# A sparse two-layer graph attention kernel: one transposition or one projection per step, with the copies a step later, and two runs of chunks as one access

## The chip, the cores and the metric

The kernel runs on 1 core of one Trainium2 chip. The core has a matrix engine (TensorE, PE in the profile; its weight loads are PEld), a vector engine (VectorE, DVE), an activation engine (ScalarE, ACT), a general engine (GpSimd, POOL) and a queue for plain transfers (SyncE, SP). Each works through its own instructions in the order in which the program issues them, and waits for others by semaphores. The metric is device time in microseconds (us) for the whole program.

## The reference

4096 nodes with 512 features; a random adjacency whose rows thin out from node 0 on. Twice: graph attention, a residual and a layernorm.

```
def attention(x, W, a):            # 8 heads of 64, or one of 512
    h = x @ W                      # per head
    e = leaky_relu(f_dst[:, None] + f_src[None, :], 0.2)
    e = where(adj > 0, e, -inf)
    return softmax(e) @ h

x = layernorm(x + attention_8(x, W0, a0))
h = elu(attention_8(x, W1, a1))              # 8 heads, concatenated
h = elu(attention_1(h, Wo, ao))              # one head of 512
x = layernorm(x + relu(h @ lin1_w + lin1_b) @ lin2_w + lin2_b)
```

Below, layer 1 and layer 2 are the two attentions of 8 heads, layer 3 is the attention of one head with the two dense products behind it. Everything is computed in fp32.

## The kernel before, in words

The nodes are cut into 32 tiles of 128. A first phase (to about 312 us of the span) turns the adjacency into lists: for each tile but the first, its edges are sorted into chunks of 128 (one edge per partition), with a source row to gather and a target node in the tile. It also projects the input for layer 1. A dense version of the program stands by for graphs that do not fit the lists; it does not run here.

Each attention reads a table in DRAM: one row per node, with its projected features and its scores. `heads_layer` (L1679) runs layers 1 and 2. Its loop (L1767) goes over *units* of up to 6 chunks; one pass is a *step*. A tile has one to five units; light tiles (17 to 31) and heavy ones (1 to 16) alternate. For a unit:

- `gather` (L1340): GpSimd issues one indirect DMA per chunk, five units ahead.
- `weights` (L1429): VectorE adds the target's and the source's scores into `z` and takes the leaky relu (L1442 to L1445), ScalarE writes two exponentials, `g` and `wp` (L1447, L1456). A unit has one or two runs of neighbouring chunks, and each run had its own instruction (`pick`, L1298). `wp` has one PSUM buffer, so that its exponential waits until the scaling of the unit before has read it.
- `scale` (L1487): VectorE builds the masks `sm` of edges against nodes (L1507 in layers 1 and 2, one instruction for each half of the tile) and multiplies the gathered rows by `wp` (L1526).
- `sum` (L1528): TensorE adds the unit's rows into the tile's accumulator (L1548).

Tile 0 is nearly full and is done densely: `First.make` (L1596) prepares one block of 128 source nodes on ScalarE (2 + 8 + 8 activations, L1607 to L1612), `sort_out` masks it on VectorE (L1620), `add` sums two blocks on TensorE (L1634) at the first step of every second tile (`taken`, L1776). These sums are called F here, and the time from one F to the next a *cycle*: 14 of them in a layer, most with one light and one heavy tile. A block's rows are loaded on the SP queue (L1592).

When a tile's units are summed, it goes through a chain of its own, kept in the list `ways`: `divide` (VectorE: reciprocal, product, and the residual with the layernorm's statistics in layer 1; ScalarE: two small activations of the layernorm, or in layer 2 two exponentials of elu, L1656 and L1657), `norm` (VectorE finishes; TensorE transposes the tile, 4 matmuls, L714; ScalarE copies the transposed tile to `xt`, 4 activations with their accumulators, L717), `project` (TensorE, L726: two halves into two PSUM tiles `ph`), `rows` (ScalarE copies the halves to `hrow`, L753, and the scores, L760; a store to the next table on the SP queue, L754). `row_of_s` (L778) spreads the scores of tile 0 over all partitions for the next layer; its `make` needs them. `split` prepares scores for the next layer. The transposed tile `pt` and the two halves `ph` share one tag with two PSUM buffers, so a transposition needs a buffer that `rows` has read out, and a projection one that the copies of `xt` have read out.

Short names for these pieces, used from here on: T (transposition), X (copies to `xt`), P (projection), H (the copies of `rows`), S (the sums of a unit), M (a `make`), N (the layernorm's two small activations).

In the loop before, a step runs `spread` and `fetch` (first step of a tile), then P, `weights` of the next unit, M, `scale`, F and `divide` (if taken), S, `gather`, H, `sort_out`, T with X, `divide`. After the loop one tile is left; `mean_of_all_but` (L798) and `finish_mean` (L818) write the mean row of the next table, then the next layer's gathers can start.

Of the kernel before, what the change touches and what calls it, by code (L numbers as in the profile page):

```python
# [11 lines left out]
F32 = mybir.dt.float32  # L12
# [4 lines left out]
AF = mybir.ActivationFunctionType  # L17
OP = mybir.AluOpType
# [4 lines left out]
P = 128  # L23
# [6 lines left out]
FC = F // P  # L30
# [10 lines left out]
HN = P // 2  # L41
# [519 lines left out]
def sparse_path(  # L561
# [24 lines left out]
    nc = tc.nc  # L586
# [16 lines left out]
    ident = const.tile([P, P], F32, name="s_ident")  # L603
# [12 lines left out]
    iota_n = const.tile([P, P], F32, name="iota_n")  # L616
# [8 lines left out]
    nl = const.tile([P, total], F32, name="nl")  # L625
# [84 lines left out]
    def turn_in(sb, ps, st, src, t):  # L710

        pt = ps.tile([P, FC, P], F32, name="pt", tag="ph")
        for c in range(FC):
            nc.tensor.transpose(pt[:, c, :], src[:, ts(c, P)], ident)  # L714
        xt = sb.tile([P, FC, P], F32, name="xt")
        for c in range(FC):
            nc.scalar.activation(  # L717
                xt[:, c, :], pt[:, c, :], AF.Copy, accum_out=st.xparts[:, c, t : t + 1]
            )
        return xt  # L720
# [559 lines left out]
    class Unit:  # L1280
# [17 lines left out]
        def pick(self, a, base=0):  # L1298

            at = 0  # L1300
            for first, n in self.runs:
                yield slice(at, at + n), a[:, first - base : first - base + n]
                at += n

    class Whole:


# [25 lines left out]
    class Attention:  # L1333
# [99 lines left out]
        def scores(self, u):  # L1433

            hs = self.st.heads
            if u.t == 0:
                return self.weights_of_first(u)
            base = parts_of(u.t)[0].first
            z = self.wk.tile([P, GC, hs], F32, name="z")[:, : u.n]
            d = by_head(u.g[:, : u.n])[:, :, :, DM] if hs > 1 else u.g[:, : u.n, F + 1 : self.st.row]  # L1440
            for at, s in u.pick(self.s[u.t], base):
                nc.vector.tensor_add(z[:, at], s, d[:, at])  # L1442
            nc.vector.scalar_tensor_tensor(z, z, ALPHA, z, op0=OP.mult, op1=OP.max)
            for at, ls in u.pick(self.ls[u.t], base):
                nc.vector.tensor_sub(z[:, at], z[:, at], ls)  # L1445
            if hs > 1:
                nc.scalar.activation(d, z, AF.Exp)  # L1447
            u.z = z
# [38 lines left out]
        def scale(self, u):  # L1487

            if u.t == 0:
                return  # L1490
            hs, n = self.st.heads, u.n
            if u.first:
                left = [sum(p.chunks[h] for p in pts if p.t == u.t) for h in range(2)]
                self.seen[u.t] = [0, 0], left

            sm = self.wk.tile([P, most_slots, HN], F32, name="sm")
            node = {k: nl[:, c : c + 1] for k, c in enumerate(u.chunks)}
            seen, left = self.seen[u.t]
            todo, at = [], 0
            for g, slots in enumerate(u.slots):  # L1500
                of_g = iota_n[:, g * HN : (g + 1) * HN]
                if hs > 1 and slots:
                    k, n_ = slots[0], len(slots)
                    c = u.chunks[k]
                    assert u.chunks[k : k + n_] == list(range(c, c + n_))
                    shape = [P, n_, HN]
                    nc.vector.tensor_tensor(  # L1507
                        sm[:, at : at + n_],
                        of_g[:, None, :].to_broadcast(shape),
                        nl[:, c : c + n_, None].to_broadcast(shape),  # L1510
                        op=OP.is_equal,
                    )
                for i, k in enumerate(slots):
                    if hs == 1:
                        nc.vector.tensor_scalar(  # L1515
                            sm[:, at + i], of_g, node[k], u.w[:, k], op0=OP.is_equal, op1=OP.mult
                        )
                    seen[g] += 1
                    todo.append((i, g, k, at + i, seen[g] == 1, seen[g] == left[g]))
                at += len(slots)  # L1520
            todo.sort(key=lambda x: x[:2])
            u.todo, u.sm = todo, sm
            if hs > 1:
                body = u.g[:, :n].rearrange("p n (h w) -> p (n h) w", w=HD)[:, :, :DM]
                wp = u.wp[:, :n].rearrange("p n h -> p (n h)")
                nc.vector.tensor_mul(body, body, wp[:, :, None].to_broadcast(body.shape))  # L1526
# [152 lines left out]
    def heads_layer(gp, wk, sb, pp, st, nxt, fetch, finish, clear):  # L1679
# [5 lines left out]
        order = [t for pair in zip(range(NT - 1, NT // 2, -1), many) for t in pair] + [1]  # L1685
# [5 lines left out]
        with tc.tile_pool(name=f"ha_{st.name}", bufs=2, space=PSUM, reuse_waits="tile") as pacc, \  # L1691
# [3 lines left out]
            at = Attention(st, gp, wk, pacc, one, whole)  # L1695
            extra = {}
            if clear:
                for i in range(GB):
                    g = gp().rearrange("p k f -> p (k f)")
# [21 lines left out]
            def divide_first():  # L1721
                at.inverse(sb, 0)
                o = at.normal(sb, 0, spare())
                finish(o, 0, extra.pop(0))()
                return norm, 0, o, lambda: None
# [4 lines left out]
            def divide(t):  # L1730
                at.inverse(sb, t)
                o = at.normal(sb, t)
                return norm, t, o, finish(o, t, extra.pop(t))

            def norm(t, o, rest):
                rest()
                xt = turn_in(pp, ps, nxt, o, t)
                return project, t, xt

            def project(t, xt):  # L1740
# [13 lines left out]
            def split(lo, n):  # L1754
                split_s(pp, nxt, lo, n)

            def run(of):

                mine = [way for way in ways if way[0] is of]
                for way in ([w for w in mine if w[1] != 0] or mine)[:1]:  # L1760
                    ways.remove(way)
                    nxt_ = of(*way[1:])
                    if nxt_:
                        ways.append(nxt_)

            ways, out_, resting = [], set(), None
            for i, u in enumerate(units):  # L1767
                pos = order.index(u.t)
                spread = None
                if u.first and pos + 2 < NT - 1:  # L1770
                    spread = at.spread(order[pos + 2])
                    extra[order[pos + 2]] = fetch(order[pos + 2])
                run(project)
                if i + 1 < len(units):
                    at.weights(units[i + 1])
                taken = u.first and first.sorted - first.summed >= min(DB, NT - first.summed) > 0  # L1776
                if i > 0:
                    first.make(i)
                held = None
                at.scale(u)  # L1780
                first.take()
                if taken:
                    first.add(DB)
                    held = divide(order[pos - 1]) if pos > 0 else None
                    if first.summed == NT:
                        extra[0] = fetch(0, spare())
                        resting = i + 2
                at.sum(u)
                if i + GB < len(units):
                    at.gather(units[i + GB])  # L1790
                late_split = [way for way in ways if way[0] is split]
                run(rows)
                run(row)
                if first.sorted < first.made - 1 or first.made == NT:
                    first.sort_out()
                run(norm)
                if held:
                    ways.append(held)
                elif u.first and pos > 0:
                    ways.append((divide, order[pos - 1]))  # L1800
                    run(divide)
                if i == resting:
                    ways.append(divide_first())
                if spread:
                    spread()
                if late_split:
                    run(split)
            assert resting and resting < len(units) - 4
            assert all(way[0] is split for way in ways)
            ways.append((divide, order[-1]))  # L1810
            run(divide)
            mrow = mean_of_all_but(pp, ps, nxt, order[-1])
            while ways:
                for of in (project, rows, row, split, norm, divide):
                    run(of)
                    if of is rows and len(out_) == NT:
                        finish_mean(ps, nxt, mrow)

# [3 lines left out]
    with ExitStack() as pools:  # L1822
        big = pools.enter_context(tc.tile_pool(name="eb", bufs=1))
        sb = pools.enter_context(tc.tile_pool(name="es", bufs=2))
        ps = pools.enter_context(tc.tile_pool(name="ep", bufs=1, space=PSUM))
        pp = pools.enter_context(tc.tile_pool(name="eq", bufs=2, space=PSUM))
# [85 lines left out]
    pp = layers.enter_context(tc.tile_pool(name="lp", bufs=2, side="right", reuse_waits="tile"))  # L1912
# [30 lines left out]
    with tc.tile_pool(name="ta", bufs=2, space=PSUM, reuse_waits="tile") as pacc, \  # L1943
# [9 lines left out]
        order = [t for block in blocks for t in block]  # L1953
        units = units_of(order)
        units[:1] = units[0].cut(2)
        at = Attention(st2, lambda: keep.tile([P, GC, F + HS], F32, name="g"), wk, pacc, ps)
# [379 lines left out]
```

## Time and profile before

| | us |
|---|---|
| median of 9 runs (lowest to highest) | 1931.04 (1928.01 to 1933.0) |
| the profiled execution | 1925.58 |
| its span, first to last instruction | 1923.8 |

| engine | busy us | share of the span |
|---|---|---|
| TensorE, matmuls | 1627.5 | 85% |
| VectorE | 1354.1 | 70% |
| GpSimd | 999.1 | 52% |
| ScalarE | 909.1 | 47% |

The span falls into the lists (0 to about 312 us), layer 1 (to 778), layer 2 (to 1208) and layer 3. In layer 1 TensorE is busy 384.5 of 466 us and VectorE 394.4; in layer 2 TensorE 366.0 of 430 us and VectorE 315.6. The mean clock granted to TensorE is 0.935 of full speed over the span.

In groups of instructions, "x1536 | 393.2, 410" means 1536 records, 393.2 us in all, 410 ns each; one matmul of the program shows as several records. In a timeline a line gives the start in us, the time from the first start to the last end of a merged run, the engine, the line of the program, and in brackets how long the engine stood idle before and who released it. Ends of matmuls are modelled, and runs of them overlap a little.

### The profile page before, as it was taken

How to read it: one execution, taken by the hardware profiler on the slowest of the kernel's cores; microseconds unless marked ns; L12 is line 12 of the kernel's file. 1: busy time of each engine (PE TensorE's matmuls, PEld its weight loads, DVE VectorE, ACT ScalarE, POOL GpSimd, SP SyncE). 2: the span in 40 equal slices, each digit the busy share in tenths (PEclk: the TensorE clock that was granted, in tenths of full speed). 3: DMA queues.
4: the chain of work that ended last, by engine and by line, in shares of the span. 5: the costliest groups of instructions: out<-in, count | busy, mean ns of one | idle time of the engine just before them, and what ended most of it. 6: DMA issues, size and time to landing. Idle time of an engine off the chain costs nothing.

```text
span 1923.8 us, 31095 instructions
## 1 busy us (share of the span) xinstructions
PE 1627.5 (85%) x9797; PEld 1205.9 (63%) x9797; DVE 1354.1 (70%) x3537; ACT 909.1 (47%) x3294; POOL 999.1 (52%) x1336
## 2 busy tenths in 40 slices
PE   4998877788988887688898988589899998899987
PEld 1675555566666665356666665366678666667776
DVE  6787666889898888388887776245665766656665
ACT  5986877555455645276666653112223131222311
POOL 5556565766665563477776563644405454535100
PEclk8999988789998998789999999789899999999999
DMA  9798873767776665467776663744545544435111
GB/s 327 282 333 312 290 269 118 224 201 214 213 230 196 203 192 175 132 179 198 196 200 185 181 164 110 240 112 116 145 142 158 131 121 140 109 119 154 56 45 35
DMA packets 140084, 343.69 MB, mean 179 GB/s; under 512 B 39525, under 2 KB 44653, under 8 KB 132230
## 3 DMA queue, kind: packets, MB, share of 16 engines
q0 software_dynamic: 64064, 180.85, 34.4%
q1 hardware_dynamic: 74246, 156.57, 23.5%
q10 hardware_dynamic: 1600, 4.19, 0.6%
q8 instruction: 80, 1.31, 0.3%
q14 instruction: 94, 0.77, 0.1%
HBM read 332.19 MB, written 42.24 MB: 195 GB/s over the span
## 4 chain that ended last, share of the span: by engine, by line
PE 40%; DVE 15%; issue 12%; POOL 10%; ACT 8%; DMA 6%; POOLq 0%; DVEq 0%; ACTq 0%; SPq 0%
PE ph L726 10%; PE acc L1548 10%; POOL g L1350 9%; DMA g<-table_t,idx 6%; DVE g L1526 3%; PE acc L1634 3%; PE px L2063 3%; PE px L2071 2%; PE py L2063 2%; ACT w L1610 2%; PE pz L2063 2%; ACT rows L1612 1%; PE py L2071 1%; PE acc L1478 1%; PE pz L2071 1%
## 5 line engine op out<-in xcount | busy, mean ns | idle before, releaser
L1350 POOL DMA_INDIRECT g<-table_t,idx x774 | 815.5, 1054 | 620.2 <-PE acc L1548 271.5
L1548 PE MATMUL acc<-g,sm 128*64 128x260 f32 (+2 forms) x3408 | 466.0, 406 | 106.9 <-DVE sm L1515 55.2
L1548 PEld LDWEIGHTS acc<-g,sm 128*64 128x64 f32 x3408 | 266.2, 144 | 269.7 <-DVE sm L1515 75.6
L726 PE MATMUL ph<-sw_t,xt 128*128 128x264 f32 (+1 forms) x1536 | 393.2, 410 | 35.5 <-ACT xt L717 28.7
L726 PEld LDWEIGHTS ph<-sw_t,xt 128*128 128x128 f32 x1536 | 303.2, 202 | 105.7 <-ACT xt L717 40.5
L1526 DVE TENSOR_TENSOR g<-g,wp 128x2048 f32<-128x2048 f32 (+5 forms) x114 | 291.8, 2560 | 1.9 <-ACT wp L1456 1.9
L717 ACT ACTIVATE xt<-pt 128x128 f32<-128x128 f32 x256 | 67.0, 276 | 197.2 <-PE pt L714 197.2
L1610 ACT ACTIVATE w<-s_row,d 128x128 f32<-128x128 f32 x512 | 155.8, 387 | 0.0
L1634 PE MATMUL acc<-rows,w 128*128 128x65 f32 x1024 | 125.3, 283 | 12.3 <-ACT rows L1612 12.3
L1634 PEld LDWEIGHTS acc<-rows,w 128*128 128x128 f32 x1024 | 125.2, 201 | 15.0 <-ACT rows L1612 12.8
L1158 DVE MAX8 cand<-key 128x8 f32<-128x85 f32 (+51 forms) x395 | 99.8, 317 | 44.2 <-PE key L992 44.1
L1612 ACT ACTIVATE rows<-rows 128x64 f32<-128x64 f32 x512 | 128.6, 334 | 0.0
L977 ACT ACTIVATE sg<-raw,value 128x2048 bf16<-128x2048 int32 x60 | 120.1, 2008 | 4.3 <-DMA raw<-in_adj_dram 3.9
L2077 ACT ACTIVATE shid<-shid,sl1b 128x256 f32<-128x256 f32 x112 | 50.6, 500 | 118.3 <-DVE shid L2015 118.3
L1667 ACT ACTIVATE rstd<-mv,s_eps 128x1 f32<-128x1 f32 x64 | 18.9, 295 | 143.8 <-DVE mv L1664 143.8
L714 PE MATMUL pt<-s_ident,o 128*128 128x128 f32 x248 | 42.7, 297 | 48.2 <-ACT ss_t L760 48.2
L1620 DVE SCALAR_TENSOR_TENSOR w<-w,mask 128x1024 f32<-128x1024 f32 x64 | 77.6, 1214 | 7.6 <-ACT w L1610 7.6
L1658 DVE SCALAR_TENSOR_TENSOR o<-ex,o 128x512 f32<-128x512 f32 x63 | 43.4, 689 | 52.5 <-ACT ex L1657 52.5
L1656 ACT ACTIVATE ex<-o 128x512 f32<-128x512 f32 x63 | 39.6, 629 | 76.1 <-DVE o L1574 67.4
L714 PEld LDWEIGHTS pt<-s_ident,o 128*128 128x128 f32 x248 | 27.3, 146 | 74.6 <-ACT ss_t L760 58.4
L1515 DVE TENSOR_SCALAR sm<-iota_n,nl,w 128x64 f32<-128x64 f32 x284 | 68.7, 318 | 0.0
L1459 ACT ACTIVATE w<-z 128x4 f32<-128x4 f32 (+4 forms) x56 | 11.6, 206 | 115.1 <-DVE z L1445 108.6
(284 smaller groups left out, 2824.7 us busy)
## 6 DMA issues: line engine op xcount, KB each, us to landing
raw<-in_adj_dram SPq DMA_DIRECT2D x60, 1024.0 KB, 7.9
table_t<-hrow SPq DMA_DIRECT2D x64, 260.0 KB, 4.0
rows<-table_t SPq DMA_DIRECT2D x64, 260.0 KB, 4.1
xr<-in_x_dram SPq DMA_DIRECT2D x63, 256.0 KB, 4.9
g<-table_t,idx POOLq DMA_INDIRECT x774, 3.8
table_t<-hrow SPq DMA_DIRECT2D x32, 257.0 KB, 4.6
xr<-sx_d SPq DMA_DIRECT2D x32, 256.0 KB, 3.1
out_dram<-xr SPq DMA_DIRECT2D x32, 256.0 KB, 2.8
```

Source lines behind the costliest of these rows:

```text
L726: nc.tensor.matmul(ph[:n], columns(c), st.w[:, c, j], start=(c == 0), stop=(c == FC - 1))
L977: nc.scalar.activation(sg[:, ts(i, w)], raw[:, ts(i, w)], AF.Sign, bias=values["half"])
L1158: nc.vector.max(out=cand[:, at : at + 8], in_=key[:, j - w0_ : j - w0_ + n_])
L1350: nc.gpsimd.indirect_dma_start(out=u.g[:, k, : self.st.row], out_offset=None, in_=self.st.table[:, :], in_offset=bass.IndirectOffsetOnAxis ...
L1526: nc.vector.tensor_mul(body, body, wp[:, :, None].to_broadcast(body.shape))
L1548: nc.tensor.matmul(out_[g * HN : (g + 1) * HN], sm[:, slot], rows(k), start=start, stop=stop)
L1610: nc.scalar.activation(w[:, h], self.st.s_row[:, h], AF.Exp, scale=0.8, bias=d8[:, h : h + 1])
L1612: nc.scalar.activation(rows[:, h, :DM], rows[:, h, :DM], AF.Copy, scale=rows[:, h, DM : DM + 1])
L1620: nc.vector.scalar_tensor_tensor(w, w, 1.0, mask0[:, self.turns[b], None, :].to_broadcast([P, HS, P]), op0=OP.max, op1=OP.mult)
L1634: nc.tensor.matmul(acc[:, j, k * HD : (k + 1) * HD], w[:, h], rows[:, h * HD : (h + 1) * HD], start=(b == lo and k == 0), stop=(b == hi - ...
L2063: nc.tensor.matmul(out_[:, m], a[:, c, ts(k, P)], b[:, c], start=m == 0 and c == 0, stop=k == ks[-1] and c == 1,)
L2071: nc.tensor.matmul(out_[:, :HF], a[:, k, ts(r, P)], b[:, k], start=k == 0, stop=k == 3)
```

## The change

Three things change; line numbers in the diff are those of the old and new file.

1. The chain of a tile in `heads_layer`. `norm` only transposes; the copies to `xt` are a stage of their own, `turned`. In a step, `turned`, `rows` and `row` come after the next unit's weights and the make, ahead of `scale`. Behind the step's sums comes either one projection or, if none is ready, one transposition. `make_room` keeps at most one tile waiting for its transposition: when a tile is about to be divided and another still waits, it runs the outstanding `rows` and `turned` and transposes, in the same step. In steps that take two blocks of tile 0 it is called between F and S. After the loop, what is left is drained.
2. The input rows for the residual (`fetch`) are asked for at the end of a tile's first step, behind the spread, and not at its start.
3. Where a unit has two runs of chunks, the additions and subtractions on `z` (all three layers) and the masks `sm` (layers 1 and 2, where each half of the tile has its own run) are one instruction with one more dimension (`both_runs`).

```diff
+    def both_runs(a, u, base=0):
+        (one, n), (two, m) = u.runs
+        assert n == m and two > one
+        v = a[:, one - base : one - base + n]
+        step, lanes, *rest = [list(x) for x in v.ap][1], v.ap[0], *[list(x) for x in v.ap][2:]
+        return bass.AP(v.tensor, v.offset, [list(lanes), [step[0] * (two - one), 2], step, *rest])
...
+            if len(u.runs) == 2:
+                z_, d_ = (a.rearrange("p (r k) h -> p r k h", r=2) for a in (z, d))
+                nc.vector.tensor_add(z_, both_runs(self.s[u.t], u, base), d_)
+            else:
+                for at, s in u.pick(self.s[u.t], base):
+                    nc.vector.tensor_add(z[:, at], s, d[:, at])
...
+            whole_ = hs > 1 and len(u.runs) == 2
+            if whole_:
+                k = n // 2
+                shape = [P, 2, k, HN]
+                nc.vector.tensor_tensor(
+                    sm[:, :n].rearrange("p (g k) w -> p g k w", g=2),
+                    iota_n.rearrange("p (g w) -> p g w", g=2)[:, :, None, :].to_broadcast(shape),
+                    both_runs(nl, u)[:, :, :, None].to_broadcast(shape),
+                    op=OP.is_equal,
+                )
...
             def norm(t, o, rest):
                 rest()
-                xt = turn_in(pp, ps, nxt, o, t)
+                pt = ps.tile([P, FC, P], F32, name="pt", tag="ph")
+                for c in range(FC):
+                    nc.tensor.transpose(pt[:, c, :], o[:, ts(c, P)], ident)
+                return turned, t, pt
+
+            def turned(t, pt):
+                xt = pp.tile([P, FC, P], F32, name="xt")
+                for c in range(FC):
+                    nc.scalar.activation(
+                        xt[:, c, :], pt[:, c, :], AF.Copy, accum_out=nxt.xparts[:, c, t : t + 1]
+                    )
                 return project, t, xt
...
+            def make_room():
+                made = False
+                while sum(way[0] is norm for way in ways) > 1:
+                    while run(rows):
+                        pass
+                    while run(turned):
+                        pass
+                    run(norm)
+                    made = True
+                return made
...
                     spread = at.spread(order[pos + 2])
-                    extra[order[pos + 2]] = fetch(order[pos + 2])
-                run(project)
                 if i + 1 < len(units):
                     at.weights(units[i + 1])
...
                     first.make(i)
-                held = None
+                late_split = [way for way in ways if way[0] is split]
+                run(turned)
+                run(rows)
+                run(row)
+                held, made_room = None, False
                 at.scale(u)
                 first.take()
                 if taken:
                     first.add(DB)
+                    made_room = make_room()
                     held = divide(order[pos - 1]) if pos > 0 else None
...
                 at.sum(u)
                 if i + GB < len(units):
                     at.gather(units[i + GB])
-                late_split = [way for way in ways if way[0] is split]
-                run(rows)
-                run(row)
                 if first.sorted < first.made - 1 or first.made == NT:
                     first.sort_out()
-                run(norm)
+                if not made_room and not run(project):
+                    run(norm)
                 if held:
                     ways.append(held)
                 elif u.first and pos > 0:
+                    make_room()
                     ways.append((divide, order[pos - 1]))
                     run(divide)
                 if i == resting:
+                    make_room()
                     ways.append(divide_first())
                 if spread:
                     spread()
+                    extra[order[pos + 2]] = fetch(order[pos + 2])
...
-            assert all(way[0] is split for way in ways)
+            make_room()
             ways.append((divide, order[-1]))
             run(divide)
+            while any(way[1] != order[-1] for way in ways if way[0] in (norm, turned)):
+                for of in (project, rows, row, split, norm, turned):
+                    while run(of, False) and of in (rows, turned):
+                        pass
             mrow = mean_of_all_but(pp, ps, nxt, order[-1])
             while ways:
-                for of in (project, rows, row, split, norm, divide):
-                    run(of)
+                for of in (project, rows, row, split, norm, turned, divide):
+                    while run(of, False) and of in (rows, turned):
+                        pass
```

More of the change, by code (lines that the diff above doesn't have):

```diff
@@ L1440, in scores @@
             d = by_head(u.g[:, : u.n])[:, :, :, DM] if hs > 1 else u.g[:, : u.n, F + 1 : self.st.row]
-            for at, s in u.pick(self.s[u.t], base):
-                nc.vector.tensor_add(z[:, at], s, d[:, at])
-            nc.vector.scalar_tensor_tensor(z, z, ALPHA, z, op0=OP.mult, op1=OP.max)
-            for at, ls in u.pick(self.ls[u.t], base):
-                nc.vector.tensor_sub(z[:, at], z[:, at], ls)
+            if len(u.runs) == 2:
[4 more added lines that the diff above has]
+                    nc.vector.tensor_add(z[:, at], s, d[:, at])
+            nc.vector.scalar_tensor_tensor(z, z, ALPHA, z, op0=OP.mult, op1=OP.max)
+            if len(u.runs) == 2:
+                nc.vector.tensor_sub(z_, z_, both_runs(self.ls[u.t], u, base))
+            else:
+                for at, ls in u.pick(self.ls[u.t], base):
+                    nc.vector.tensor_sub(z[:, at], z[:, at], ls)
             if hs > 1:
@@ L1499, in scale @@
             todo, at = [], 0
+            whole_ = hs > 1 and len(u.runs) == 2
+            if whole_:
+                k = n // 2
+                assert u.slots == [list(range(k)), list(range(k, n))]
+                shape = [P, 2, k, HN]
[5 more added lines that the diff above has]
+                )
             for g, slots in enumerate(u.slots):
                 of_g = iota_n[:, g * HN : (g + 1) * HN]
-                if hs > 1 and slots:
+                if hs > 1 and slots and not whole_:
                     k, n_ = slots[0], len(slots)
@@ L1755, in split, with run @@
                 split_s(pp, nxt, lo, n)
-            def run(of):
+            def run(of, waits=True):
                 mine = [way for way in ways if way[0] is of]
-                for way in ([w for w in mine if w[1] != 0] or mine)[:1]:
+                for way in ([w for w in mine if w[1] != 0 and waits] or mine)[:1]:
                     ways.remove(way)
@@ L1764, in run @@
                         ways.append(nxt_)
+                    return True
+                return False
+            def make_room():
[8 more added lines that the diff above has]
+                return made
             ways, out_, resting = [], set(), None
```

## The prediction

> **What bounds the kernel now.** I read the page's busy table first (TensorE busy 85%, no other engine over 70%), then the waits of the stretch that holds the two layers of 8 heads (312 to 1208 us of the span), then busy time by stage, then the timeline of one cycle. Short names as in the section on the kernel: T transposes, X the copies `xt`, P projections, H the copies of `rows`, S a step's sums, F the sums of tile 0, M a `make`, N the two small activations of a layernorm.
>
> The waits, longest in total first (engine, line, what it waited for; us, times, longest):
> ```profile
> ACT xt L717 <- PE pt L714: 197.2, 59, 8.4
> ...
> PE pt L714 <- ACT ss_t L760: 48.2, 22, 3.5
> ...
> PE ph L726 <- ACT xt L717: 28.7, 61, 2.5
> ```
> TensorE waits at T until H has freed a PSUM buffer, 22 times 2.2 us, and at P for X, 61 times 0.47 us. ScalarE's 197 us are mere idleness: it has nothing to do until T is done.
>
> Busy time in stretches cut at starts of F: cycles 1-5 and 6-11 of layer 1, then of layer 2 (the columns are length, PE, PEld, DVE, ACT, POOL, granted clock, DMA):
> ```profile
> 376.30:512.80 136.50, 114.43 (x750) 84.75 (x749) 119.85 (x255) 77.92 (x369) 90.35 (x85) 0.91 0.72 216
> 512.80:666.70 153.90, 133.43 (x907) 99.97 (x906) 133.49 (x274) 85.68 (x412) 89.16 (x86) 0.94 0.70 203
> ...
> 840.50:960.40 119.90, 106.78 (x750) 79.69 (x749) 100.99 (x192) 81.81 (x361) 88.49 (x85) 0.97 0.72 198
> 960.40:1099.20 138.80, 126.20 (x907) 95.45 (x906) 111.22 (x211) 93.78 (x415) 93.05 (x87) 0.99 0.68 185
> ```
> Cycles 6-11 last 25.65 us each in layer 1 and 23.1 in layer 2, with 22.2 and 21.0 us of TensorE work. VectorE has 22.2 us in layer 1: no cycle there gets much shorter than 22. One wait of layer 1, on TensorE and then on ScalarE:
> ```profile
> 499.92 1.97 PE L1548 MATMUL acc<-g,sm 128*64 128x260 f32 x16 [0.17 <-DVE g L1526]
> 505.37 1.11 PE L714 MATMUL pt<-s_ident,o 128*128 128x128 f32 x4 [3.48 <-ACT ss_t L760]
> ...
> 506.94 6.03 PE L726 MATMUL ph<-sw_t,xt 128*128 128x264 f32 x16 [0.22 <-ACT xt L717]
> ```
> ```profile
> 500.04 0.20 ACT L1607 ACTIVATE d<-rows 128x8 f32<-128x8 f32 x1
> 500.27 0.22 ACT L1608 ACTIVATE rows<-rows 128x8 f32<-128x8 f32 x1
> 500.40 2.43 ACT L1610 ACTIVATE w<-s_row,d 128x128 f32<-128x128 f32 x8
> 502.73 2.00 ACT L1612 ACTIVATE rows<-rows 128x64 f32<-128x64 f32 x8
> 504.64 0.62 ACT L753 COPY hrow<-ph 128x260 f32<-128x260 f32 x2
> 505.16 0.21 ACT L760 COPY ss_t<-ph 128x4 f32<-128x4 f32 x2
> ```
> T waits for H because H stands behind a whole M (4.6 us) in ScalarE's queue. And the wait is paid twice: the P after it takes 6.03 us instead of 3.83; the granted clock over 499-513 us is 0.76, against 1.00 over 486-499. In layer 1 nine such P took 5.05 to 6.03 us (mean 5.52, +1.7), after waits of 1.74 and of 2.61 us or more; after 1.99 and 2.26 us P kept 3.83. In layer 2 three of the eight waits near 1.8 us slowed P, to 5.3-5.4 (+1.6).
>
> **The change, part by part.** No matmul and no activation is added or removed; copies and projections move. The order in which the changed program issues on each engine shows where to, for cycles 6-11 of both layers (three steps, two tiles): TensorE A: F T S; B: S P T; C: S P. ScalarE A: M H N; B: X H N; C: M X. Before it was TensorE A: P F S; B: S T; C: P S T, ScalarE A: M N H; B: X N; C: M H X. So T no longer meets P at once, but two things are new. In step B room has to be made, so H is issued in the step of its own P, and ScalarE must wait for the end of that P. In step C, X stands behind M, and P behind X. What is queued behind: N (in layer 2 the two exponentials of elu), M, X.
>
> *Cycles 6-11.* From the end of P in B to the start of P in C, in layer 2, each from start to start in the timeline: the rest of H and elu 1.64 (0.11 after P ends, 1179.30 to 1180.83), the step's exponentials with M 4.86 (908.99 to 913.85), the first X to P 0.42 (907.98 to 908.40): 6.92 us. Layer 1: H 0.50, N 0.42, M 4.90 (478.55 to 483.45), X 0.42: 6.24. TensorE has for it only T (0.46 to 0.5 wait, 0.6 work) and S of 1.93 to 2.8 us. It stands 3.9 us (3.1 with the long S) in layer 2, 3.2 (2.35) in layer 1. The loop closes: 6.92 + P 3.66 + scores 0.15 + F 3.62 + T 0.55 + S 2.78 + scores 0.38 + S 1.92 + P 3.66 = 23.64 us; layer 1, with P 3.70, 23.04. The longer S of five of the six cycles add 4.3 in all. Layer 1: 6 x 23.04 + 4.3 = 142.5, against 153.9: -11.4. Layer 2: 146.1 against 138.8: +7.3. T in A is covered: M and H end 6.2 us after P starts, P and F take 7.5.
> The clock comes on top. Layer 1: waits of 3.2 us slow P, those of 2.35 lie between the rows 2.26 (not) and 2.61 (did), so half: 3.8 x 1.7 = 6.5, -4.9 in all (ends: none -11.4, all six -1.2). Layer 2: 5.5 x 1.63 = 9.0, +16.3 (ends +7.3, +17.1).
> The Trainium skill ("TensorE: Matmul & The Clock Gate", "What's actually happening") has the clock fall to half only after an idle window of about 3.4 us. The rows above, slowed after 1.74 and 2.61 us, disagree. By the rule layer 1 would pay nothing here and layer 2 two waits of six, and the whole sum below would be 12 us less, a gain of 8; I go by the rows.
>
> *Cycles 1-5.* The deeper pipeline does two T and two P fewer here (8 of each, not 10): -8.6 per layer, due later. Waits and slow P before: 31.3 us in layer 1, 16.5 in layer 2 (read off the TensorE timeline, cycle by cycle). After: each cycle still has one T behind M H, or P behind M X: 2.95 to 3.0 us in layer 1, as M can start only when VectorE's scaling of that step is done (5.9 us after the previous S; M and H 5.55 more; TensorE reaches the end of S at 8.45), plus 2.1 for two short ones and 7.9 of slow P: 25. Layer 2: 1.35 to 2.35 a cycle, 1.7 once, slow P 3: 14.5. So -14.9 and -10.6 (ends: each wait as before, -8.6; half of them, -21 and -16).
>
> *Cycle 12 to the last S.* One T and one P of the deferred two return, +4.3; `row_of_s` goes behind the last S (layer 1: -3.9 with its waits at 748-752 us; layer 2 -0.5); waits at P, -3 and -2. In layer 1 ScalarE also waits for a load of `rows` for the next layer (3.8 us, S then 7.44). Its three loads (L1592) now stand behind two stores L1935 on the SP queue, the second of which needs tile 0's layernorm, about 4.7 us later; I take +3. Sums: +0.9 after rounding, and +2.3 (ends -5, +6 each).
>
> *Layer ends.* From the last S to the first gather of the next layer it is now 17.9 us (773.65 to 791.58). After: T of the last tile at 5.0 (divide, layernorm), mean projection 5.8 to 9.5, P of tile 0 to 13.2, H and diagonals 15.1, two `row_of_s` with copies to 18.8, P of the last tile to 22.5, its copies 23.7 (a make's w and rows stand between them), mean row 25.5, gather 28.1: +10.2. The first make needs `row_of_s` too, so three makes (14 us) come after; the first S moves from +28.9 to about +45, but the third and fourth were waiting for gathers, which come 10.2 later anyway. Layer 2, worked the same way, one `row_of_s`: 14.6 to 21.4, +6.8. Ends: +4 to +15, +3 to +9.
>
> *Runs as one access.* 72 z additions, 72 subtractions and 48 masks fewer. A pair of z takes 0.31 us from start to start, a single one of 32 elements 0.22 to 0.25: below 0.1 us each, 13 to 18 us of VectorE in all. In layers 1 and 2 it lies in slack, 0. In layer 3, where TensorE waits 55 us for `sm` (L1515), 24 units x 0.18 x half: -2 (ends -6, 0).
> *Fetch moved* behind the spread's end: needed two tiles later, 20 us against 4.9 us landing: 0. If that cover went, a wait of 5 us at one addition.
>
> **Sum.** Layer 1: -14.9 - 4.9 + 0.9 + 10.2 = -8.7. Layer 2: -10.6 + 16.3 + 2.3 + 6.8 = +14.8. Layer 3: -2. Total +4.1 on the profiled 1925.6, 1929.7. The median lies 5.5 above that execution: 1935.
>
> **Rivals.** (A, faster) The new waits leave the clock alone, because the T and S between the two idle pieces count as work. For it: 1.99 and 2.26 us did not slow P. Against: all waits of 2.6 us or more did. Price: -6.5 - 9.0 - 7.9 - 3.0 = -26: 1909. It decides from 1.7 us per slow P downwards: at 0.9 the sum is -10.
> (B, slower) The layer ends cost in full: what moves behind the last S shortens nothing before it, since the end of the loop is set by VectorE's layernorm and the 7.44 us load wait (+4.3 twice), and layer 2 starts with its makes (+14.6 for +10.2). For it: ScalarE's wait for that load. Against: TensorE is busy 84% from 666 to 774 us. +13: 1948.
> (C) The change does not do what it says: projections still follow copies at once. The issue order rules it out.
>
> **Chances.** Forecast 0.55, its own range 1925 to 1945; A 0.22; B 0.23. Range over all, with the ends above taken as independent (about 18 us each way): 1914 to 1955. A difference under 0.2% (3.9 us) can't be told from none. The forecast splits 0.31 slower, 0.16 same, 0.08 faster; so slower 0.54, same 0.16, faster 0.30.
>
> **What would show it.** P waiting for X some 3 to 4 us in step C of cycles 6-11, ScalarE idle before H in step B; cycles of layer 1 near 24 us, of layer 2 near 25; waits of T for H nearly gone there; granted clock of layer 2 below 0.97; first gather of layer 2 near 28 us after the last S. Wrong, if P in step C waits less than 2 us: then ScalarE ran ahead, and the kernel is faster.

## The result and the profile after

| | before | changed |
|---|---|---|
| median, us | 1931.19 (31 runs) | 2222.78 (10 runs, 2214.38 to 2227.4) |
| ratio, with its 95% interval | | 1.1509 (1.1493 to 1.1524) |
| profiled execution, us | 1925.58 | 2226.9 |
| its span, us | 1923.8 | 2225.2 |
| TensorE busy, us | 1627.5 | 1711.6 |
| mean granted clock | 0.935 | 0.882 |

The changed kernel is 15% slower, and the forecast of 1935 us (1914 to 1955) is far off. No matmul was added: TensorE's longer busy time goes with the lower clock. So some 300 us of the span is new waiting and what it costs in clock.

First the groups of instructions of the changed kernel, with the line that did not stand out before (busy us, mean ns | idle time of the engine just before, and what ended it):
```profile
L1593 DVE TENSOR_TENSOR o<-acc,rd_t 128x512 f32<-128x512 f32 x62 | 42.9, 691 | 331.0 <-DMA sx_d<-o 190.2 <-PE pt L1765 137.7 <-PE acc L1574 2.5
```
and the same instruction in the kernel before:
```profile
L1567 DVE TENSOR_TENSOR o<-acc,rd_t 128x512 f32<-128x512 f32 x62 | 42.8, 691 | 2.1
```
This is the product of `divide`, which writes a tile's normalized sums into `o`. VectorE now stands 331 us in front of it, and 2.1 before. It waits for nothing that it reads: it waits for the store of x1 out of `o` (190 us, layer 1) and for T reading `o` (138 us), that is, for a *buffer* of `o` to come free. There are two.

The waits of the two layers of 8 heads in the changed kernel (312 to 1500 us; us in total, times, longest) show what stands behind it:
```profile
POOL g L1358 <- PE acc L1574: 395.2, 63, 16.2
PEld acc L1574 <- DVE g L1552: 218.5, 47, 12.4
PE acc L1574 <- DVE g L1552: 205.1, 45, 12.1
DVE o L1593 <- DMA sx_d<-o: 190.2, 21, 13.7
ACT wp L1471 <- DVE g L1552: 173.5, 80, 3.6
ACT rstd L1693 <- DVE mv L1690: 163.0, 25, 11.4
...
DVE o L1593 <- PE pt L1765: 137.7, 23, 8.7
...
PE acc L1574 <- DVE o L1593: 47.6, 20, 7.4
```
VectorE works in order. While the product waits, the next unit's scaling of the gathered rows (L1552) waits behind it; S waits for the scaling (205 us, 34 before) or, as in the step below, for the product itself (47.6 us), and the gathers for the buffers that S reads (395 us, 84 before). T's wait for H, 48.2 us before, is 19.9 us. The wait that the prediction looked at became small, and a far larger one appeared on an engine whose order it had not followed.

Busy time by stage, cut at starts of F as before (length, PE, PEld, DVE, ACT, POOL, granted clock, DMA): cycles 1-5 and 6-11 of layer 1, then of layer 2.
```profile
380.48:524.73 144.25, 107.74 (x712) 77.58 (x709) 107.91 (x211) 71.64 (x332) 88.16 (x85) 0.87 0.66 194
524.73:794.16 269.43, 156.18 (x910) 108.03 (x908) 132.46 (x256) 89.91 (x422) 85.00 (x85) 0.77 0.41 117
...
1029.16:1159.32 130.16, 109.38 (x711) 79.75 (x709) 91.29 (x157) 78.62 (x333) 89.59 (x86) 0.86 0.67 184
1159.32:1360.18 200.86, 143.77 (x910) 103.44 (x908) 109.27 (x184) 97.57 (x414) 85.81 (x84) 0.87 0.47 125
```
Cycles 6-11 take 44.9 us each in layer 1 (25.65 before) and 33.5 in layer 2 (23.1 before), with the same VectorE work. They are +115.5 and +62.1 us of the +301.4; from cycle 12 to the last S it is +42.7 and +30.9, between the layers +18.5, cycles 1-5 +7.7 and +10.3, the rest (start, end of layer 2, layer 3) +13.7. At a granted clock of 0.77 the same matmuls take 156 us where they took 133.

One step of layer 1, from the timeline (start, us, engine, in brackets the idle time before and who ended it):
```profile
566.97 0.55 DVE L1701 TENSOR_SCALAR o<-o,mv,rstd 128x512 f32<-128x512 f32 x1
...
567.43 0.20 DVE L1581 RECIPROCAL rd_t<-acc 128x8 f32<-128x8 f32 x1
...
569.67 2.00 ACT L1638 ACTIVATE rows<-rows 128x64 f32<-128x64 f32 x8
...
570.42 3.77 PE L1660 MATMUL acc<-rows,w 128*128 128x65 f32 x32
...
571.58 0.62 ACT L753 COPY hrow<-ph 128x260 f32<-128x260 f32 x2
...
572.23 0.32 SPq L754 DMA_DIRECT2D table_t<-hrow  x1
572.64 1.89 SPq L1618 DMA_DIRECT2D rows<-table_t  x2
...
574.02 0.61 PE L1765 MATMUL pt<-s_ident,o 128*128 128x128 f32 x4
...
574.63 0.38 SPq L1994 DMA_DIRECT2D sx_d<-o  x1
...
581.33 0.69 DVE L1593 TENSOR_TENSOR o<-acc,rd_t 128x512 f32<-128x512 f32 x1 [13.70 <-DMA sx_d<-o]
...
582.07 5.44 PE L1574 MATMUL acc<-g,sm 128*64 128x260 f32 x24 [7.44 <-DVE o L1593]
```
The old tile's layernorm is finished at 567.52, and VectorE is ready for the product at 567.63. Its buffer still holds the tile two before it. T of that tile stands behind F on TensorE and ends at 574.63. Its store stands on the SP queue behind the table's store, which waits for H, which stands behind a make on ScalarE, and behind two loads of rows into the buffers that F reads. The second load starts at 574.22, when F ends; the store leaves at 574.63 and has landed 6.6 us later. In a step without F no load stands between: the store at 595.71 leaves directly behind a table's store at 595.30. After the wait, 24 matmuls of S take 5.44 us where they took 2.85 before. In layer 2 nothing is stored, and the product waits for T alone: 12 times in cycles 6-11, 89.5 us in all.

The Trainium skill ("Perfetto Trace Analysis", Optimization Strategy) reads a gap that repeats over a stretch, on the engine that should be saturated, as a possible lack of SBUF or PSUM for the next tile. The trace bears it out with one difference: the engine that should be saturated, TensorE, names the scaling as what it waits for, and the missing buffer is found one step further back, on VectorE in front of L1593.

### The profile page after: what moved, and what is told of

The parts are those of the page before. It is cut to its first block, busy times and chain, and to the rows that moved or that the text cites. A ratio compares the mean times of both kernels' runs of the same rounds, so it can differ in the third digit from the quotient of the medians.

```text
span 2225.2 us, 30980 instructions
## 1 busy us (share of the span) xinstructions
PE 1711.6 (77%) x9797; PEld 1240.8 (56%) x9797; DVE 1337.9 (60%) x3345; ACT 922.5 (41%) x3294; POOL 992.4 (45%) x1336
## 5 line engine op out<-in xcount | busy, mean ns | idle before, releaser
L1574 PE MATMUL acc<-g,sm 128*64 128x260 f32 (+2 forms) x3408 | 543.9, 460 | 338.1 <-DVE g L1552 205.1
L1574 PEld LDWEIGHTS acc<-g,sm 128*64 128x64 f32 x3408 | 297.7, 163 | 536.8 <-DVE g L1552 218.5
L726 PE MATMUL ph<-sw_t,xt 128*128 128x264 f32 (+1 forms) x1536 | 384.1, 403 | 30.7 <-ACT xt L1771 23.3
L726 PEld LDWEIGHTS ph<-sw_t,xt 128*128 128x128 f32 x1536 | 297.2, 198 | 120.2 <-ACT xt L1771 38.1
L1552 DVE TENSOR_TENSOR g<-g,wp 128x2048 f32<-128x2048 f32 (+5 forms) x114 | 291.9, 2561 | 9.1 <-ACT wp L1471 9.1
L1593 DVE TENSOR_TENSOR o<-acc,rd_t 128x512 f32<-128x512 f32 x62 | 42.9, 691 | 331.0 <-DMA sx_d<-o 190.2
L1660 PE MATMUL acc<-rows,w 128*128 128x65 f32 x1024 | 137.4, 298 | 16.6 <-ACT rows L1638 16.6
L1660 PEld LDWEIGHTS acc<-rows,w 128*128 128x128 f32 x1024 | 133.3, 214 | 18.0 <-ACT rows L1638 17.5
L753 ACT COPY hrow<-ph 128x260 f32<-128x260 f32 (+2 forms) x128 | 44.7, 370 | 145.1 <-PE ph L726 145.0
L1471 ACT ACTIVATE wp<-z 128x32 f32<-128x32 f32 (+5 forms) x114 | 23.9, 210 | 173.6 <-DVE g L1552 173.5
```

The lines of the kernel that those rows point to most:

```text
L726: nc.tensor.matmul(ph[:n], columns(c), st.w[:, c, j], start=(c == 0), stop=(c == FC - 1))
L1574: nc.tensor.matmul(out_[g * HN : (g + 1) * HN], sm[:, slot], rows(k), start=start, stop=stop)
L1660: nc.tensor.matmul(acc[:, j, k * HD : (k + 1) * HD], w[:, h], rows[:, h * HD : (h + 1) * HD], start=(b == lo and k == 0), stop=(b == hi - ...
```

## The experiments

### Three buffers of o, and four

The changed kernel with one buffer more. The room in SBUF for it comes from elu's `ex`, which shares the buffers of `xr` (layer 2 uses no `xr`).

```diff
-                o = sb.tile([P, F], F32, name="o")
+                o = sb.tile([P, F], F32, name="o", bufs=3)
...
     def elu(sb, o):
-        ex = sb.tile([P, F], F32, name="ex")
+        ex = sb.tile([P, F], F32, name="ex", tag="xr", bufs=3)
```

> The changed kernel with three buffers for o instead of two (the room comes from elu's ex sharing the buffers of xr, which layer 2 does not use). Theory (VectorE's product waits for a buffer of o, and all else follows from that): the 331 us of idle time before the product fall below 20, the cycles 6-11 fall from 45 and 33 us to about 24 and 25, and the time falls to the forecast, 1914 to 1955 us. Rival (ScalarE in step with the projections, the copies xt behind a make, or the two PSUM buffers set the longer cycles): the time stays above 2150 us and the waits move to other lines.

Measured: 1976.43 us, ratio to before 1.0237 (1.019 to 1.0284). In the group of the product:
```profile
L1593 DVE TENSOR_TENSOR o<-acc,rd_t 128x512 f32<-128x512 f32 x62 | 42.9, 692 | 8.3 <-DMA sx_d<-o 6.2
```
331 us have become 8.3, and 2222.8 - 1976.4 = 246 of the 292 us lost are back. Cycles 6-11 in the windows of this kernel:
```profile
508.54:660.11 151.57, 128.63 (x911) 95.51 (x908) 133.24 (x256) 86.28 (x413) 90.95 (x85) 0.98 0.71 209
...
976.55:1130.41 153.86, 132.62 (x910) 99.33 (x908) 111.24 (x184) 94.68 (x414) 89.91 (x87) 0.93 0.63 168
```
25.3 and 25.6 us each. The buffer was the main cause, as the theory said. But the time is 21 us above the upper end of the forecast's range: the theory held for the cycles 6-11 and not for the rest.

> As before with four buffers of o. Theory: make_room keeps at most one tile ahead of its transposition, so a third buffer is all that can be used: within 6 us of the kernel with three. If the product with three still waits for a store or a transposition, four are faster by that wait, 10 us or more. Rival (ScalarE or PSUM): above 2150 us as with three.

Measured: 1972.75 us, 1.0211 (1.0162 to 1.026). The same as with three.

The control for the shared `ex`, with two buffers of `o`:

> A control: the changed kernel with two buffers of o, and elu's ex in the buffers of xr, as the kernels with three and four buffers of o have it. If the sharing itself does nothing, 2210 to 2235 us; if it does part of what the third buffer seemed to do, less.

Measured: 2218.33 us in one run, inside the 2214 to 2227 us of the changed kernel. Sharing is not what the 246 us come from.

### The store of x1 no longer behind the table's store

```diff
-        nc.sync.dma_start(st.table[t * P : t * P + n, :], hrow)
+        nc.scalar.dma_start(st.table[t * P : t * P + n, :], hrow)
```

> The changed kernel, two buffers of o, with the table's store issued by ScalarE behind its copies instead of on the SP queue, so that the store of x1 no longer stands behind it. Theory: in layer 1 the 21 waits of the product for the store of x1 (190 us, 9.1 each) fall to some 4 to 5 each, the landing time of such a store; 85 to 110 us less in layer 1, nothing in layer 2: 2110 to 2150 us. Rival (the landing of the store itself or the late transposition is what counts, not the queue): within 20 us of 2223.

Measured: 2186.43 us, 1.1319 (1.1274 to 1.1364): 36 us less where 85 to 110 were expected. Why is seen in what the product waited for:
```profile
  PE pt L1765: 207.2, 35
  DMA sx_d<-o: 85.0, 10
```
The 21 waits for the store fell to 10 and from 190 to 85 us, but those for T rose from 23 to 35 and from 138 to 207. Two things are behind this. In steps without F, seven products from the start of cycle 6 into cycle 12 now wait 46.7 us in all, for T, where they waited 71.4 for the store: T and the store held the same buffer to nearly the same moment, and freeing it of one leaves the other. A wait is put down to the last of several, and what is won by removing that one is the distance to the next. The seven products in steps with F in the same stretch won nothing (78.3 us for 79.6), for there the table's store was not what held the store of x1. It still stands behind the loads of rows, which wait for F:
```profile
565.59 3.77 PE L1660 MATMUL acc<-rows,w 128*128 128x65 f32 x32
567.64 2.10 SPq L1618 DMA_DIRECT2D rows<-table_t  x2
569.19 0.61 PE L1765 MATMUL pt<-s_ident,o 128*128 128x128 f32 x4
569.83 0.44 SPq L1994 DMA_DIRECT2D sx_d<-o  x1
575.32 0.69 DVE L1593 TENSOR_TENSOR o<-acc,rd_t 128x512 f32<-128x512 f32 x1 [12.04 <-DMA sx_d<-o]
```
In these seven steps the store leaves 0.4 to 0.6 us after the end of F in both kernels.

### The two small parts alone

The kernel before with `both_runs` and the later `fetch`, nothing else.

> The kernel before with only the two small parts of the change: two runs as one access, and the fetch behind the spread. My steps: 0 to -6 us, so 1925 to 1933. Rival (one access over two runs is slow, or the fetch comes late): 1950 or more.

Measured: 1933.1 us, 1.0009 (0.9993 to 1.0025). No difference. There are 192 VectorE instructions fewer and 11.6 us less VectorE work (1342.5 us busy for 1354.1), which does not show in the time, and a later fetch costs nothing that can be seen. The two were not tried apart.

### What is left with three buffers: the copies to xt ahead of the make

```diff
+                run(turned)
                 if i + 1 < len(units):
                     at.weights(units[i + 1])
...
                     first.make(i)
                 late_split = [way for way in ways if way[0] is split]
-                run(turned)
                 run(rows)
```

> Three buffers of o, and the copies to xt issued first in the step, ahead of the next unit's weights and of the make. Theory (what is left of the loss inside the loops is the forecast's term: P waits for copies that stand behind a make): the waits of P for xt (67 us on weight loads, 25 of them) fall below 20 us, cycles 6-11 of layer 2 fall from 25.6 us to about 23, and the time from 1976 to 1940-1960 us. Rival (the projection waits in any case, since the forced transposition comes late or VectorE sets the cycle): 1970 us or more.

Measured: 1963.16 us, 1.0173 (1.0144 to 1.0201), 13 us less than with three buffers alone, where 16 to 36 were expected. TensorE's waits, of the kernel with three buffers and then of this one:
```profile
PE ph L726 <- ACT xt L1771: 55.4, 22, 3.8
...
PE pt L1765 <- ACT ss_t L760: 17.5, 18, 3.5
```
```profile
PE acc L1574 <- DVE g L1552: 70.5, 29, 6.7
PE pt L1765 <- ACT ss_t L760: 38.8, 31, 3.5
```
P's wait for X is gone from the list, but T waits 21 us more for H: two makes now follow each other on ScalarE, in step C and in step A, and H of the projection between them stands behind both.

### The same, and H between the two halves of a make

```diff
-        def make(self, step=0):
+        def make(self, step=0, between=lambda: None):
...
                 nc.scalar.activation(w[:, h], self.st.s_row[:, h], AF.Exp, scale=0.8, bias=d8[:, h : h + 1])
+            between()
             for h in range(HS):
...
-                    first.make(i)
+                    first.make(i, lambda: run(rows))
```

> The changed kernel with three buffers of o, the copies to xt first in the step, and the copies of the projected rows between the two halves of the make. Theory (what kept the kernel with the copies first at 1963 is T behind F waiting for H behind two makes, 31 waits and 39 us, and the slow matmuls after them): these waits fall below 20 us and the time to 1930-1948 us. Rival (two tiles per cycle do not fit three steps, the forced transposition with H in P's own step and the ends of the layers are what is left): 1955 us or more.

Measured: 1925.74 us, 0.9967 (0.9949 to 0.9986). T's waits for H, scores and rows together, are 15.3 us. Cycles 6-11 of layer 2 fall from 25.6 us to 22.0 and keep the clock:
```profile
948.52:1080.48 131.96, 124.31 (x911) 93.33 (x908) 114.09 (x189) 95.26 (x421) 99.48 (x92) 1.00 0.71 202
```
Layer 1 stays at 25.3; why is not shown (TensorE's waits for the scaling are 82.4 us in all, 59.5 with three buffers alone). The edits together undo the whole loss of 292 us: 246 by the buffer of `o`, 51 by the order of X, H and the makes on ScalarE. Part of the 51 is no cost of the change, since T's wait for H behind a make was in the kernel before too.

### Tile 0 first

With three buffers, in `run`:

```diff
-                for way in ([w for w in mine if w[1] != 0 and waits] or mine)[:1]:
+                for way in ([w for w in mine if w[1] == 0] or mine)[:1]:
```

> Three buffers of o, and tile 0 taken ahead of the other tiles wherever one is chosen from the list of pending work, so that its row of scores is spread inside the loop and not behind the last sums. Theory (the longer layer ends, from the last sums of layer 1 to the first of layer 2 now 49.7 us against 28.9, come from the row of scores and two projections that wait behind the last sums): that stretch falls to 35-42 us, the time to 1955-1968 us. Rival (the end is set by the last tile's own chain and the mean row): within 5 us of 1976.

Measured: 1973.74 us, 1.0212 (1.0175 to 1.0249), not distinguishable from 1976. The stretch without S between the layers did fall, from 49.7 to 37.1 us. But the last S of layer 1 starts at 779.4 instead of 768.8, and the first S of layer 2 at 818.5 instead of 820.5. What was taken out of the gap lengthened the loop before it. The mechanism expected was there and the price was not.

### The aim of the change by order alone

The kernel before has the wait that the forecast started from: T for H, which stands behind a make. Here only the make is cut, in steps without F: first half (`w`), H, second half (scaled rows).

```diff
...
+                late_split = [way for way in ways if way[0] is split]
                 if i > 0:
-                    first.make(i)
+                    first.make(i, lambda: None if taken else run(rows))
...
```

> The kernel before, with the copies of the projected rows issued between the two halves of a make in steps that take no block of tile 0; nothing of the change. It tries the aim of the change by order on ScalarE alone. Theory (T waits for H only because H stands behind a whole make): the 22 waits of T (48 us, 2.2 each) fall below 15 us, the slow projections behind them too, and the time falls to 1896-1920 us. Rival (P then waits for the copies of xt, which now stand behind the second half of the make, or VectorE sets the cycle anyway): 1925 us or more.

Measured: 1899.15 us, 0.9828 (0.9793 to 0.9863). T's wait for H falls from 48.2 to 7.6 us, P's wait for X rises from 28.7 to 51.1, since X now stands behind the second half. Next, that half is issued only behind X, at the end of the step (`make` hands it back as `half`):

```diff
...
-                    first.make(i, lambda: None if taken else run(rows))
+                half = first.make(i) if i > 0 else None
+                if not taken:
+                    run(rows)
+                elif half:
+                    half()
...
                 run(norm)
+                if half and not taken:
+                    half()
```

> The kernel before with a make cut in two in steps that take no block of tile 0: its first half (weights w), then the copies of the projected rows, and its second half (scaled rows) only behind the copies to xt, at the end of the step. Theory (what cutting the make gained is partly paid back, P waits for xt 51 us instead of 29 since these copies stand behind the second half): the wait of P falls back to about 29 us and the time from 1899 to 1875-1892 us. Rival (the second half then delays the next step's exponentials, or VectorE sets the cycle in layer 1): 1896 us or more.

Measured: 1879.44 us, 0.9728 (0.9689 to 0.9767). TensorE's waits in its two layers:
```profile
PE ph L726 <- ACT xt L717: 24.2, 61, 0.6
PE pt L714 <- ACT ss_t L760: 13.3, 13, 1.6
```
and cycles 6-11 of layer 1, 23.4 us each where they were 25.65, at 0.99 of the clock:
```profile
495.13:635.27 140.14, 127.62 (x906) 95.87 (x905) 135.16 (x278) 87.76 (x421) 91.88 (x88) 0.99 0.76 230
```
This is the fastest version found, 2.7% under the kernel before. The Trainium skill ("Perfetto Trace Analysis", Optimizing Scalar/DVE Operations) advises to break up instructions of ScalarE or VectorE where these are not saturated but cause bubbles on other engines. Here no instruction was broken up, only a run of 18 of them, and that was enough: ScalarE, busy 47% of the span before, had held TensorE 48.2 us at T, and holds it there 13.3 us now. With the two small parts of the change on top:

> The same, with two runs as one access and the fetch behind the spread. The kernel before did not gain from these two (1933). Theory: with shorter cycles VectorE is nearer to the bound in layer 1, so its 13 to 18 us less work show in part: 0 to 6 us less than without. Rival: nothing, within 3 us.

Measured: 1880.52 us, 0.9747 (0.9707 to 0.9787): still nothing.

## Why the prediction was wrong

- **The step that failed** is "T in A is covered: M and H end 6.2 us after P starts, P and F take 7.5". For TensorE that is right. But T was priced only by what TensorE does next, never by what its end releases. `make_room` puts T of one tile immediately ahead of `divide` of another, and that `divide` writes into the buffer T reads: with two buffers, tile t takes that of tile t-2, and before the change T of tile t-2 had ended long before: at the product at 519.56 us by 13 us (T at 505.37), at the next, at 533.40, by 10 (T at 522.27). VectorE entered the cycles 6-11 as a total only ("VectorE has 22.2 us in layer 1"); no term stands for an instruction of it that waits for a buffer. The missing term is 246 us, the step from two buffers to three, of the 288 by which the forecast missed. The other 41 (1976 against 1935) are terms of the wrong size, below.
- **The SP queue.** The moved step issues a DMA too, the store of x1. The prediction followed the stores L1935 only to the loads of rows at the layer's end, not to the buffer that the store holds. Taking the store out from behind the table's store brought 36 us: in steps without F T holds the buffer nearly as long, and in steps with F the store stands behind the loads of rows, which wait for F. How much the store costs with T and these loads out of the way was not tried.
- **Cycles 6-11.** With three buffers the forecast's own case exists, and its terms can be read: -2.3 us in layer 1 (forecast -4.9) and +15.1 in layer 2 (+16.3). P in step C waits 2.4 and 3.1 us on average, 6 times in each layer (forecast 2.35 to 3.2, and 3.1 to 3.9). The waits were foretold rightly, the cost in clock was not: 2 of these P were slowed in layer 1 and 3 in layer 2, where 3.8 and 5.5 stood in the sum, by 1.7 us each in layer 1 as assumed, but by 2.9 in layer 2 and not 1.63. That 8.8 us came out for 9.0 in layer 2 is luck. In layer 1 the rest without the clock is -5.7 us and not -11.4. All this was hidden under a larger wait: in the changed kernel itself P waits for X only 23.3 us in 16 waits in all, while VectorE stands and sets the pace.
- **Cycles 1-5** were mis-sized: with three buffers -7.5 and +2.8 us, not -14.9 and -10.6. Four pieces fewer are there (711 and 712 matmul records for 750), yet TensorE's busy time in layer 2 is 105.2 us for 106.8, at a clock of 0.90 for 0.97. The forecast had counted 3 us of slow P there; three P were slowed, by 6.2 us in all.
- **Cycle 12 to the last S** is +3.7 and +10.7 us with three buffers (forecast +0.9 and +2.3): the deferred pieces come back here.
- **Layer ends.** From the end of the last S to the first gather it is 33.0 us with three buffers (before 17.9, forecast 28.1) and 22.7 (before 14.7, forecast 21.4). The order of the pieces was as foretold, T of the last tile at 5.2 us for 5.0; but the mean projection took 5.56 us for 3.7, after TensorE had stood 4.59 us; that is 2 of the 5 us missing in layer 1, the others are not traced.
- **The small parts**: 0 forecast, 0 found, and the -2 us in layer 3 did not show in the run of these parts alone.
- **The sums.** Three steps of the working do not come out as written, none by more than 2 us: the terms from cycle 12 on add up to +0.4 and +1.8, not +0.9 and +2.3; one wait of 3.2 us and half of five of 2.35 make 3.5 slow P, not 3.8; and at 0.9 us per slow P the sum is about -8, not -10.
- **Rivals.** A (the clock is left alone) fell: with three buffers 10 of the 12 projections that had waited 2.5 us or more for X were slow. B (layer ends in full) was nearer, and still more than twenty times too small (+13 us) for the changed kernel. None of the cases had the mechanism that decided, so the range could not hold it.
- **The signs named**: T's wait for H did fall (48 to 20 us), the clock of layer 2 did fall below 0.97. These came true beside a cause that they do not test; the length of the cycles, near 24 and 25 us by the forecast, is the sign that spoke, at 45 and 33. The sign of being wrong came true too: no P of cycles 6-11 waits more than 1.4 us in the changed kernel. But what was read into it, "the kernel is faster", did not follow; a likely reason, not tested, is that the copies had more time in a longer cycle.

## What to carry to other kernels

Moving a step later moves the release of everything it reads: list the buffers of its inputs, count how many tiles are alive between writer and last reader (the DMAs out of it included), and compare with the pool. A writer that waits for a buffer shows as idle time before an instruction all of whose inputs are ready, released by a reader of its *output* tile. Before deferring a stage so as to let a slow queue run ahead, try cutting the long block in that queue: here the wait of T was cut from 48.2 to 13.3 us by putting the copies of H between the halves of a make and the second half behind X, for 2.7%, with no deeper pipeline.

## What the runs showed of the hardware

- TensorE pays for short waits. Of the projections with three buffers of `o`, 10 of 12 that had waited 2.9 to 3.8 us for X took over 5 us instead of 3.7 to 3.8, and 1 of 8 that had waited 0.7 to 2.5 us. Two waits of the same length differ: after 2.94 us P took 3.73 us at 997.11 and 6.69 us at 1047.78. In the fastest version no P waits over 0.6 us for X, and the granted clock in cycles 6-11 is 0.99 and 1.00.
- One VectorE access over two runs costs a little less than two. The records alone say too much, an addition on z over twice 16 columns 210 ns and two single ones 177 ns each, because two in a row overlap: from the start of the first to the end of the second it is 274 ns in the median. For a mask over twice 128 columns it is 485 ns for the pair and 418 for the one. So some 60 ns are saved each time, and over the 192 instructions 11.6 us of VectorE's busy time. The time did not move for it in either kernel to which it was added.
